# Layer 0 of a four-layer vision network: part of the second feed-forward product, the input transposes and the late norm are issued earlier within a strip

## The chip, the cores and the metric

The kernel runs on one core of a Trainium2 chip. The metric is the device time of one execution in microseconds (us); less is better. Each engine of the core works through its own queue of instructions in order: PE (TensorE, with PEld for its weight loads), DVE (VectorE), ACT (ScalarE), POOL (GpSimd) and SP (SyncE, which here issues most of the DMAs).

## The reference

Four layers run one after the other; each adds its result to its input. Everything is float32. The change touches layer 0 alone, a block with a depthwise convolution, a Mamba-2-like state-space mixer and a feed-forward part on 8 images of 64 x 64 positions and 192 channels:

```python
x = x + _L0_conv_ref(_gn(x), ...)     # layer 0: this case
x = x + _L1_conv_ref(_gn(x), ...)     # layer 1: four selective scans
x = x + _L2_conv_ref(_gn(x), ...)     # layers 2 and 3: 3x3 depthwise convolutions
x = x + _L3_conv_ref(_gn(x), ...)
```

Within layer 0, `_gn` normalizes over groups of 6 channels and the whole image, so its statistics are complete only when all of an image has been read. What follows, for each image:

- a 3x3 depthwise convolution, added to its input (conv1), and a layer norm over the channels (norm1);
- a projection to a gate z (384 columns), to x, B and C (512 columns) and to a time step dt for each of 6 heads (the "steps"); x, B and C pass a causal convolution over 4 positions and a silu, dt a softplus;
- the state-space sum in chunks: within a chunk `scores = (C B^T) * exp(seg) * dt` times x, and a state that is carried from chunk to chunk;
- the gate silu(z), an RMS norm and a projection back to 192 channels, added to the stream;
- a second 3x3 convolution (conv2), a second layer norm (norm2), and the feed-forward part: 192 to 768 channels, gelu, 768 to 192 channels, added.

## The kernel before, in words

**Tiling.** An image is cut into 8 strips of 512 positions (`NCH` = 8, `NJ` = 512); 8 images give 64 strips. Channels lie on the partitions as 2 groups of 96, positions in the free dimension. The chunk of the state-space sum is 128 positions, so a strip has 4 chunks (`NB` = 4).

**A pipeline over strips.** The loop at the end of `layer0` runs over q, and one turn of it (here "a strip") works on several strips at once, each at another stage: the first convolution and norm of strip q+1, the state-space part of strip q, the second convolution and norm of strip q-2, and the feed-forward part of strip q-3. The input of a strip nine ahead is transposed in the same turn (`take_in`, L237).

**What sets the order.** PE, DVE, ACT and POOL run in the order in which the Python code emits instructions; the order of SP's DMAs is left to the framework. The stages are generators that emit some instructions and then yield. `together` (L147) takes one step of each generator in turn, round after round, until those in its list are done; generators under `beside` get a step per round but aren't waited for. A generator that is listed twice gets two steps per round. So where a yield stands, and which generators are listed together, is the schedule.

**A turn has three phases.**

1. `widen` (first feed-forward product and gelu, L636), `project_xbc` (the x, B, C projection and its causal convolution, L387) and `project_out` of the strip before (L599), `conv1` (L314) and `residual` (L657) together. ACT needs the gelu table.
2. `gates` (L416): four matmuls of the gate projection, each with a silu on ACT, then the silu of B, C and x (L436 to L438), with one step of `conv2` (L629) per round beside them. ACT needs the silu table.
3. `exp_and_ln` loads a third ACT table (L693), and then `front` and `back` (the state-space part, chunk by chunk: L510 and L546), `narrow` (second feed-forward product, L664), the rest of `conv2`, and the chain `norms`: norm1, steps, norm2 and `take_in`, one after the other, two steps of it per round.

`norm2` can't begin before conv2 of its strip is done; it yields until then.

**Names and lines.** In `take_in`, L243 loads the input (SP), L249 transposes it (PE), L251 copies (ACT) and L252 takes bn_stats (DVE) of each half, L254 writes it out (SP); after the last strip of an image come the group norm's statistics (L259 to L276: bn_aggr, two small matmuls L263 and L271, a reciprocal root). `layer_norm` (L333) transposes to rows (L344), takes bn_stats (L349), computes 1/sqrt through Ln and Exp on ACT and four small DVE operations (`rsqrt`, L165 to L170), writes normalized rows (L357, ACT), transposes back (L369) and scales (L371). `steps` (L441) multiplies (L449), computes the softplus on ACT (L467 to L469), multiplies for cumulative sums (L477, L478), writes them to DRAM (L484) and reads them back broadcast to 128 partitions (L496); the relu of L506 in `exponents` reads these. In `front`, L524 to L527 transpose and multiply for a chunk, L529 is an exp, L532 copies x to positions on the partitions, L538 to L540 scale it on POOL, L541 multiplies the score matrix M. In `back`, L563 and L565 multiply with the state, L567, L570 and L571 update it, L574 and L576 multiply with M, L585 to L587 gate and square. In `narrow`, L677 multiplies six times for each half of the output channels into the one buffer of the PSUM bank "fc", L680 adds bias and residual (DVE, tile `xo`), L681 takes bn_stats, L682 stores (a DMA issued by POOL).

PSUM banks come from small rings by `bank`: two for "tp", two for "mm", three for "y", one for "fc". A matmul that would overwrite a bank waits until its last reader is done.

Of the kernel before, what the change touches and what calls it, by code (L numbers as in the profile page):

```python
# [15 lines left out]
B, H, W, C = 8, 64, 64, 192  # L16
# [10 lines left out]
NCH = L // NJ  # L27
# [119 lines left out]
def together(*threads, beside=()):  # L147

    threads = list(threads)
    while threads:  # L150
        for t in list(threads) + list(beside):
            if next(t, threads) is threads and t in threads:
                threads.remove(t)
# [20 lines left out]
def layer0(ctx: ExitStack, tc, a, dr, x, x1, mv1, cst):  # L174
# [58 lines left out]
    def at(q):  # L233
        return 0 <= q < len(strips)


    def take_in(b, r):  # L237
        if b >= B:
            return
        if r == 0:  # L240
            st0[b] = mk(pool, [CP, CT, NCH, 6], "st0")
        xt = mk(pool, [128, NB, C], "xt", bufs=2)
        nc.sync.dma_start(xt, x[b].rearrange("(g j p) c -> g p j c", p=128, j=NB)[r])  # L243
        xc = mk(pool, [CP, CT, NJ], "xc", bufs=2)
        yield
        for ct in range(CT):
            ps = bank("tp")[:CP]
            for j in range(NB):
                nc.tensor.transpose(ps[:, j * 128 : (j + 1) * 128], xt[:, j, ct * CP : (ct + 1) * CP], ident)  # L249
            yield  # L250
            nc.scalar.copy(xc[:, ct, :], ps)  # L251
            nc.vector.bn_stats(st0[b][:, ct, r, :], ps)  # L252
            yield
        nc.sync.dma_start(x0[b][:, :, r * NJ : (r + 1) * NJ], xc)  # L254
        if r < NCH - 1:
            return
        mv, d, q = (mk(pool, s, t) for s, t in (([CP, CT, 2], "mv0"), ([CP, CT], "gd"), ([CP, CT], "gq")))
        gm, sc, nb = (mk(pool, [CP, CT], t, bufs=2) for t in ("gm", "sc0", "nb0"))
        for ct in range(CT):  # L259
            nc.vector.bn_aggr(mv[:, ct, :], st0[b][:, ct, :, :])  # L260
        yield
        ps = bank("tp")[:CP, 0:CT]
        nc.tensor.matmul(ps, grp, mv[:, :, 0], start=True, stop=True)  # L263
        yield
        nc.vector.tensor_copy(gm, ps)
        nc.vector.tensor_tensor(d, mv[:, :, 0], gm, ALU.subtract)
        nc.vector.tensor_tensor(q, d, d, ALU.mult)
        nc.vector.tensor_tensor(q, q, mv[:, :, 1], ALU.add)
        yield
        ps = bank("tp")[:CP, 0:CT]  # L270
        nc.tensor.matmul(ps, grp, q, start=True, stop=True)  # L271
        yield
        nc.vector.tensor_scalar(q, ps, EPS, None, ALU.add)
        rsqrt(nc, pool, q, sc, "gr")
        nc.vector.scalar_tensor_tensor(nb, gm, -1.0, sc, ALU.mult, ALU.mult)
        norm[b] = sc, nb  # L276
        yield
# [96 lines left out]
    def norm1(q):  # L374
        if at(q):
            hn1[q] = mk(pool, [CP, CT, NJ], "hn1")
            yield from layer_norm(xs[q][:, :, W : W + NJ], l1w, l1b, hn1[q])

    def norm2(q):
        if at(q):  # L380
            while ("conv2", q) not in done:
                yield
            hn2[q] = mk(pool, [CP, CT, NJ], "hn2")
            yield from layer_norm(x2s[q], l2w, l2b, hn2[q])
# [31 lines left out]
    def gates(q):  # L416

        if not at(q):
            return
        zs = zss[q] = mk(pool, [128, NB, DIN], "zs")  # L420
        for i in range(NB):
            ps = bank("mm")
            for ct in range(CT):
                nc.tensor.matmul(
                    ps[:, 0:DIN],
                    hn1[q][:, ct, i * 128 : (i + 1) * 128],
                    w_zdt[:, ct, 0:DIN],
                    start=ct == 0,
                    stop=ct == CT - 1,
                )  # L430
            yield
            nc.scalar.activation(zs[:, i, :], ps[:, 0:DIN], AF.Silu)
        del hn1[q]
        cv = cvs[q]
        Bc, Cc = state["B"], state["C"] = mk(pool, [NS, NJ], "Bc"), mk(pool, [NS, NJ], "Cc")
        nc.scalar.activation(Bc, cv[0:NS, 3, :], AF.Silu)  # L436
        nc.scalar.activation(Cc, cv[NS:128, 3, :], AF.Silu)
        nc.scalar.activation(cv[:, 0:3, :], cv[:, 0:3, :], AF.Silu)  # L438
        yield
# [70 lines left out]
    def front(q, made):  # L510

        if not at(q):
            return
        dtv, E, _, _ = decays[q]
        cv, Bc, Cc = cvs[q], state["B"], state["C"]
        for i in range(NB):
            while made.get("back", 0) < i - 1:
                yield
            c0, c1 = i * 128, (i + 1) * 128
            if i + 2 < NB:  # L520
                fetch_sums(q, i + 2)
            ps = bank("mm")
            for o in range(DT):
                nc.tensor.transpose(ps[:, o * 128 : (o + 1) * 128], cv[:, o, c0:c1], ident)  # L524
            nc.tensor.transpose(ps[:, DIN : DIN + NS], Bc[:, c0:c1], ident[:NS, :NS])
            pgt = bank("mm")
            nc.tensor.matmul(pgt[:, 0:128], Bc[:, c0:c1], Cc[:, c0:c1], start=True, stop=True)  # L527
            M = made.pop(("M", i))
            nc.scalar.activation(M, M, AF.Exp, scale=-1.0)  # L529
            yield  # L530
            xb = mk(pool, [128, DIN + NS], "xb", bufs=2)
            nc.scalar.copy(xb, ps[:, 0 : DIN + NS])  # L532
            G = mk(pool, [128, 128], "G", bufs=2)
            nc.vector.tensor_tensor(G, pgt[:, 0:128], upper, ALU.mult)
            yield
            xv = split(xb[:, 0:DIN])
            xdt, xw, xd = (mk(pool, [128, DIN], t, bufs=2) for t in ("xdt", "xw", "xd"))
            nc.gpsimd.tensor_tensor(split(xdt), xv, heads(dtv[:, i, :]), ALU.mult)  # L538
            nc.gpsimd.tensor_tensor(split(xw), split(xdt), heads(E[:, 1, i, :]), ALU.mult)
            nc.gpsimd.tensor_tensor(split(xd), xv, heads(dsk), ALU.mult)  # L540
            nc.vector.tensor_tensor(M, M, G.unsqueeze(1).to_broadcast((128, NH, 128)), ALU.mult)  # L541
            made[i] = xb, xdt, xw, xd, M
            exponents(q, i + 1, made)
            yield
# [84 lines left out]
    def conv2(q):  # L629
        if at(q):  # L630
            x2s[q] = mk(pool, [CP, CT, NJ], "x2", bufs=2)
            yield from conv(xs[q], x2s[q], c2w, mid[:, 1, :], c2b)
            xs.pop(q - 1, None)
            done.add(("conv2", q))
# [29 lines left out]
    def narrow(q):  # L664
        if not at(q):
            return
        b, r = strips[q]
        sl = slice(r * NJ, (r + 1) * NJ)
        ff = ffs.pop(q)
        if r == 0:  # L670
            st1[b] = mk(pool, [CP, CT, NCH, 6], "st1", bufs=2)
        res = ress.pop(q)
        xo = mk(pool, [CP, CT, NJ], "xo")
        for ct in range(CT):
            ps = bank("fc")[:CP]
            for o in range(6):
                nc.tensor.matmul(ps, f2w[:, o, ct * CP : (ct + 1) * CP], ff[:, o, :], start=o == 0, stop=o == 5)  # L677
                if ct > 0 or o > 1:
                    yield
            nc.vector.scalar_tensor_tensor(xo[:, ct, :], ps, f2b[:, ct : ct + 1], res[:, ct, :], ALU.add, ALU.add)  # L680
            nc.vector.bn_stats(st1[b][:, ct, r, :], xo[:, ct, :])  # L681
        nc.gpsimd.dma_start(x1[b][:, :, sl], xo)  # L682
        if r == NCH - 1:
            for ct in range(CT):
                nc.vector.bn_aggr(mv1[:, b, ct, :], st1[b][:, ct, :, :])
        yield

    def one_by_one(*threads):
        for t in threads:
            yield from t  # L690
# [4 lines left out]
    with every_engine(tc):  # L695
        for r in range(NCH):
            if r == NCH - 1:
                exp_and_ln()
            together(take_in(0, r))
        load_strip(0)  # L700
        for q in range(-1, len(strips) + 3):
            load_strip(q + 2)
            load_residual(q - 2)
            together(
                widen(q - 3), one_by_one(project_xbc(q), project_out(q - 1)), conv1(q + 1), residual(q - 3)
            )
            made, second = {}, conv2(q - 2)
            exponents(q, 0, made)
            together(gates(q), beside=[second])
            exp_and_ln()  # L710
            norms = one_by_one(norm1(q + 1), steps(q + 1), norm2(q - 2), take_in(*divmod(q + NCH + 1, NCH)))
            together(front(q, made), norms, narrow(q - 3), back(q, made), norms, second)


@with_exitstack
# [602 lines left out]
```

## Time and profile before

| what | value |
|---|---|
| median of 3 runs | 26190.96 us (26157.72 to 26194.59) |
| the profiled execution | 26178.77 us, of which the span of its instructions is 26177.0 us |
| PE busy | 23676.9 us, 90% of the span |
| DVE busy | 22201.3 us, 85% |
| ACT busy | 20110.8 us, 77% |
| POOL busy | 17658.9 us, 67% |
| mean granted TensorE clock | 0.948 of full speed |

The span falls into stages: layer 0 up to about 5,690 us, layer 1's input part up to 8,600, its scans up to about 23,340, its output part up to about 24,640, then layers 2 and 3. The shares of the whole span are a mean over these, and the scans hold more than half of it; what a change in layer 0 is worth is read from layer 0's own part. "idle before" behind an instruction in the views is the time in which its engine had nothing running, with the engine, tile and line that ended it. The granted clock is the share of full TensorE speed that the chip's throttle gave in a stretch; in the trace of this case it is 1.0 or 0.5 at any moment.

### The profile page before, as it was taken

The page shows a single profiled execution, that of the slowest core. Times are in us where ns is not written, and L with a number is a line of the kernel's source. Part 1 is how long each engine was busy: PE and PEld are TensorE (multiplying, and loading weights), DVE is VectorE, ACT ScalarE, POOL GpSimd, SP SyncE. Part 2 cuts the span into 40 slices and gives each one's busy share as a digit, 9 for nine tenths or more (in the row PEclk, how much of TensorE's full clock was granted, in tenths as well). Part 3 has the DMA queues.
Part 4 walks back from the last instruction along what each step waited for, and adds up shares of the span by engine and source line. Part 5 has one row for each costly group of instructions (what it writes and reads, how often), then busy time and mean ns, then how long its engine had stood idle before and what let it go on. Part 6 is the DMA issues. An engine that isn't in the chain of part 4 may idle for free.

```text
span 26177.0 us, 442405 instructions
## 1 busy us (share of the span) xinstructions
PE 23676.9 (90%) x156160; PEld 18442.5 (70%) x156160; DVE 22201.3 (85%) x25001; ACT 20110.8 (77%) x40019; POOL 17658.9 (67%) x18396
## 2 busy tenths in 40 slices
PE   7888888888899999999999999999999999987766
PEld 4444444445588888888888888888888888863322
DVE  6777777756799999999999999999999999986566
ACT  4555555544499999999999999999999999974322
POOL 2222222210199999999999999999999999972100
PEclk8888888889999999999999999999999999998878
DMA  1111111113333333333333333333333333346311
GB/s 56 42 43 42 44 41 44 35 40 115 112 101 94 97 102 94 96 103 94 96 103 94 96 102 95 95 101 96 95 100 97 95 99 97 96 143 198 120 34 29
DMA packets 1461962, 2275.55 MB, mean 87 GB/s; under 512 B 247181, under 2 KB 773133, under 8 KB 1458202
## 3 DMA queue, kind: packets, MB, share of 16 engines
q1 hardware_dynamic: 1445402, 2196.90, 28.9%
q0 software_dynamic: 14336, 50.34, 0.5%
q8 instruction: 1232, 20.19, 0.3%
q14 instruction: 992, 8.13, 0.1%
HBM read 1811.37 MB, written 435.42 MB: 86 GB/s over the span
## 4 chain that ended last, share of the span: by engine, by line
PE 37%; ACT 29%; POOL 13%; DVE 13%; issue 6%; DMA 2%; POOLq 0%; SPq 0%; DVEq 0%; ACTq 0%
ACT dA L1045 12%; POOL hc L1095 10%; PE pd L1051 6%; ACT sb L1029 6%; PE yt L984 5%; DVE h L1086 5%; ACT bd L1029 4%; PE y L643 3%; PE fc L677 3%; DVE x L71 2%; PE pd L1053 2%; DMA yin<-y 2%; PE mm L399 2%; PE mm L943 2%; PE y L576 1%
## 5 line engine op out<-in xcount | busy, mean ns | idle before, releaser
L1095 POOL TENSOR_TENSOR hc<-h,bc 128x512 f32<-128x512 f32 x12288 | 15443.8, 1291 | 477.5 <-DVE h L1086 337.3
L1086 DVE TENSOR_TENSOR_SCAN h<-dA,st,pd 128x512 f32<-128x512 f32 x10752 | 12951.9, 1262 | 533.1 <-PE pd L1051 371.8
L1045 ACT ACTIVATE dA<-dl,A_logs 128x512 f32<-128x512 f32 x12288 | 8785.3, 715 | 46.9 <-DVE h L1086 39.6
L984 PE MATMUL yt<-sq,hc 128*128 128x128 f32 x49152 | 7489.9, 275 | 203.2 <-POOL hc L1095 102.8
L1051 PE MATMUL pd<-bd,dut 128*128 128x128 f32 x49152 | 6581.5, 277 | 254.2 <-DVE h L1086 232.1
L1051 PEld LDWEIGHTS pd<-bd,dut 128*128 128x128 f32 x49152 | 5968.6, 192 | 610.1 <-PE yt L984 342.9
L984 PEld LDWEIGHTS yt<-sq,hc 128*128 128x128 f32 x49152 | 5668.5, 141 | 649.3 <-POOL hc L1095 629.2
L1029 ACT ACTIVATE sb<-dut,xt 128x384 f32<-128x384 f32 x8192 | 4762.6, 606 | 1.1 <-DVE dut L970 1.0
L1053 PE MATMUL pd<-sq,sb 128*128 128x128 f32 x24576 | 3739.6, 275 | 9.3 <-DVE h L1086 0.4
L1053 PEld LDWEIGHTS pd<-sq,sb 128*128 128x128 f32 x24576 | 2821.8, 141 | 480.5 <-DVE dl L957 380.8
L1029 ACT ACTIVATE bd<-sq,xt 128x128 f32<-128x128 f32 x8192 | 3010.2, 392 | 0.0
L1086 DVE TENSOR_TENSOR_SCAN h<-dA,pd 128x512 f32<-128x512 f32 x1536 | 1772.8, 1203 | 115.4 <-PE pd L1051 75.8
L71 DVE SCALAR_TENSOR_TENSOR x<-x,w,x 96x3969 f32<-96x3969 f32 (+1 forms) x192 | 838.3, 4366 | 486.9 <-ACT x L64 483.9
L538 POOL TENSOR_TENSOR xdt<-xb,dtv 128x384 f32<-128x384 f32 x256 | 222.2, 868 | 1366.9 <-ACT xb L532 1366.8
L413 POOL COPY halo<-raw 128x12 f32<-128x12 f32 x64 | 13.0, 202 | 1375.7 <-ACT raw L403 1375.7
L304 DVE SCALAR_TENSOR_TENSOR x<-xs,cpe_w,x 96x504 f32<-96x504 f32 (+1 forms) x1024 | 902.1, 881 | 30.1 <-ACT x L292 20.3
L826 DVE SCALAR_TENSOR_TENSOR u<-xa,conv_w,u 128x504 f32<-128x504 f32 x1152 | 850.0, 742 | 50.2 <-ACT u L818 12.5
L943 PE MATMUL mm<-xs,w_dt 13*128 13x512 f32 x1536 | 863.0, 641 | 1.8 <-DVE dl L957 1.0
L677 PE MATMUL fc<-ff,fc_w 128*96 128x512 f32 x1536 | 861.0, 677 | 2.7 <-DVE xo L680 2.7
L1097 POOL COPY st<-h 128x3 f32<-128x3 f32 x4096 | 831.1, 203 | 0.0
L304 DVE SCALAR_TENSOR_TENSOR xs<-x0h,cpe_w,xs 96x504 f32<-96x504 f32 (+1 forms) x1024 | 757.8, 745 | 23.7 <-ACT xs L292 2.5
L643 PE MATMUL y<-hn,fc_w 96*128 96x512 f32 x1536 | 750.2, 627 | 0.1
(234 smaller groups left out, 25752.7 us busy)
## 6 DMA issues: line engine op xcount, KB each, us to landing
bc<-bcd SPq DMA_DIRECT2D x4096, 256.0 KB
yin<-y SPq DMA_DIRECT2D x256, 768.0 KB
csb<-csd SPq DMA_DIRECT2D x256, 384.0 KB
dut<-ut SPq DMA_DIRECT2D x128, 768.0 KB
y<-ys SPq DMA_DIRECT2D x128, 768.0 KB
dut<-ut SPq DMA_DIRECT2D x256, 384.0 KB
y<-ys SPq DMA_DIRECT2D x256, 384.0 KB
xt<-x1d SPq DMA_DIRECT2D x128, 384.0 KB
```

What stands on the lines that cost most here:

```text
L71: nc.vector.scalar_tensor_tensor(d[:, h0:h1, w0:w1], s[:, h0 + dy : h1 + dy, w0 + dx : w1 + dx], w[:, ct, tap : tap + 1], d[:, h0:h1, w0:w ...
L304: nc.vector.scalar_tensor_tensor(d[:, :, w0:w1], s[:, dy : dy + R, w0 + dx : w1 + dx], w[:, ct, tap : tap + 1], d[:, :, w0:w1], ALU.mult, ...
L643: nc.tensor.matmul(ps, f1w[:, ct, o * 128 : (o + 1) * 128], hn2[q][:, ct, :], start=ct == 0, stop=ct == CT - 1)
L677: nc.tensor.matmul(ps, f2w[:, o, ct * CP : (ct + 1) * CP], ff[:, o, :], start=o == 0, stop=o == 5)
L943: nc.tensor.matmul(ps, w_dt[:, k, o * 128 : (o + 1) * 128], made["xs"][0 : 1 + R1, :], start=True, stop=True)
L984: nc.tensor.matmul(yt[:, t * 128 : (t + 1) * 128], src[:, t * 128 : (t + 1) * 128], mat, is_transpose=mat is ident, start=first and t == 0 ...
L1029: nc.scalar.activation(v, src, AF.Copy, scale=m["xt"][:, t, 1 + R1 + n : 2 + R1 + n])
L1045: nc.scalar.activation(dA, ready[s]["dl"][:, o, :], AF.Exp, scale=aneg[:, k, o, n : n + 1])
L1051: nc.tensor.matmul(dst, ready[s]["dut"][:, t, cols], brows[g, t], start=True, stop=True)
L1053: nc.tensor.transpose(dst, brows[g, t][:, cols], ident)
L1086: nc.vector.tensor_tensor_scan(h[:, o, rev], decay.pop(j)[:, rev], turned.pop(j)[:, rev], 0.0 if first else st[:, o, n : n + 1], ALU.mult, ...
L1095: nc.gpsimd.tensor_tensor(hc, h[:, o, :], held[g], ALU.mult)
```

## The change

Five edits, all in layer 0:

- The group norm's statistics leave `take_in` and become a generator of their own, `statistics`.
- `take_in` moves from the end of the chain `norms` to phase 2, beside `gates`.
- In phase 2, `conv2` gets two steps per round instead of one.
- `narrow` yields for the first time after four matmuls instead of three, and its first step is taken ahead of phase 3, before ACT's table load; so four of the six matmuls of its first half stand before the first matmul of `front` on PE.
- In the chain `norms`, norm2 comes before the steps, and the statistics are last.

No instruction is added or dropped. Lines after L254 shift by 3.

```diff
@@ take_in
         nc.sync.dma_start(x0[b][:, :, r * NJ : (r + 1) * NJ], xc)
-        if r < NCH - 1:
+
+    def statistics(b, r):
+
+        if b >= B or r < NCH - 1:
             return
@@ narrow
                 nc.tensor.matmul(ps, f2w[:, o, ct * CP : (ct + 1) * CP], ff[:, o, :], start=o == 0, stop=o == 5)
-                if ct > 0 or o > 1:
+                if ct > 0 or o > 2:
                     yield
@@ the loops
-            together(take_in(0, r))
+            together(one_by_one(take_in(0, r), statistics(0, r)))
...
-            made, second = {}, conv2(q - 2)
+            made, second, ff = {}, conv2(q - 2), narrow(q - 3)
+            nxt = divmod(q + NCH + 1, NCH)
             exponents(q, 0, made)
-            together(gates(q), beside=[second])
+            together(gates(q), take_in(*nxt), beside=[second, second])
+            next(ff, None)
             exp_and_ln()
-            norms = one_by_one(norm1(q + 1), steps(q + 1), norm2(q - 2), take_in(*divmod(q + NCH + 1, NCH)))
-            together(front(q, made), norms, narrow(q - 3), back(q, made), norms, second)
+            norms = one_by_one(norm1(q + 1), norm2(q - 2), steps(q + 1), statistics(*nxt))
+            together(front(q, made), norms, ff, back(q, made), norms, second)
```

## The prediction

> **What bounds the kernel now.** I read the stages first (busy time by stretch), then the TensorE waits of the stage that the change touches, then one strip of that stage instruction by instruction. The columns of the first view are length, busy us (and instructions) of PE, PEld, DVE, ACT and POOL, granted clock, DMA share, GB/s.
>
> ```profile
> 133.00:5565.00 5432.00, 4609.30 (x16322) 2482.31 (x16321) 3842.20 (x7265) 2778.42 (x5895) 1466.70 (x1704) 0.86 0.13 41
> 8600.00:23340.00 14740.00, 14314.63 (x118151) 13040.23 (x118149) 14110.91 (x12795) 14387.04 (x29073) 14384.95 (x14898) 1.00 0.34 97
> ```
>
> Layer 0 is the first line: PE 85% busy, DVE 71%, ACT 51%, and a granted clock of 0.86 where the scan stage has 1.00. The change can act in these 5,432 us alone. The issues of L484, one per strip, stand 85.4 to 87.2 us apart in 45 strips (mean 85.9), 90 to 97 in eight, seven of them with an image's statistics, and 86.4 to 91.9 (mean 90.1) in the last seven, which have no transposes left to do. What PE waits for, between 400 and 5400 us (total us, times, longest):
>
> ```profile
> PE tp L369 <- ACT lrow L357: 361.2, 58, 6.5
> PE mm L524 <- ACT cv L438: 184.0, 57, 3.2
> PE y L574 <- POOL xd L540: 68.3, 57, 1.2
> PE y L565 <- POOL xw L539: 61.9, 57, 1.1
> PE tp L615 <- ACT yc L610: 35.5, 58, 0.6
> ```
>
> Two waits recur in every strip: 6.2 us for the rows of a layer norm, 3.2 us for the silu. One strip in order of time (start, us, engine, line, operation, idle before it) shows where:
>
> ```profile
> 2521.36 0.55 PE L524 MATMUL mm<-sq,cv 128*128 128x128 f32 x3 [3.23 <-ACT cv L438]
> 2523.37 5.33 PE L677 MATMUL fc<-ff,fc_w 128*96 128x512 f32 x6
> 2528.91 1.88 PE L677 MATMUL fc<-ff,fc_w 128*96 128x512 f32 x4
> ...
> 2560.64 2.66 PE L576 MATMUL y<-xdt,M 128*128 128x64 f32 x12
> 2563.09 1.49 PE L344 MATMUL tp<-sq,x 96*128 96x96 f32 x8
> 2570.81 2.11 PE L369 MATMUL tp<-sq,lrow 128*96 128x128 f32 x8 [6.22 <-ACT lrow L357]
> 2572.93 1.94 PE L249 MATMUL tp<-sq,xt 128*96 128x128 f32 x8
> 2574.66 2.78 PE L643 MATMUL y<-hn,fc_w 96*128 96x512 f32 x4
> ```
>
> The layer norm that ends the strip has nothing beside it: L344, bn_stats, rsqrt, rows and L369 follow one another. And matmuls run at half speed around both holes: six fc records took 5.33 us after the silu wait, where four took 1.88 later. Idle in this strip is 6.22 + 3.23 + 1.24 + 1.09 + 0.61 + 0.39 = 12.8 us of 87.0. Full-speed durations summed by line (24 fc records at 0.43, 24 of L643, 16 of L399, and so on) give 67 us of TensorE work; the other 6 to 7 us are the half clock.
>
> [...]
>
> **The change, part by part**, in strip time, t = 0 at the first L643 (2487.69). Lines are those of before.
>
> *Transposes into the silu phase.* Eight L249 records (1.73 us by their starts) go between the L424 products. L424 begins at t = 25.1 (2512.80): 25.1 + 5.33 + 1.73 = 32.2. On ACT one L251 copy (0.58) fits in the 0.80 us gaps between silus; the second copy and conv2's second identity (0.81) now stand before the table load, so the first xb comes about 2.2 us later. On DVE two bn_stats (0.69 each) join the convolution. On SP the xt load and the x0 write are issued mid-strip, strips ahead of their readers: nothing.
>
> *Four of the six fc steps of the first half before the front.* 8 x 0.43 = 3.4: PE reaches L524 at t = 35.6; the silu ends at 2521.3 + 1.05 = t 34.7. The 3.2 us wait is gone.
>
> *Two conv2 steps per round beside the gates.* DVE was already behind there; its row before shows the convolution running on past the silu, and the first xo far later:
>
> ```profile
> 2517.91 3.84 DVE L304 SCALAR_TENSOR_TENSOR x<-xs,cpe_w,x 96x504 f32<-96x504 f32 x5
> 2535.46 0.75 DVE L680 SCALAR_TENSOR_TENSOR xo<-fc,fc_b,res 96x512 f32<-96x512 f32 x1 [0.31 <-PE fc L677]
> ```
>
> Ten conv2 steps now precede the first bn_stats of norm1 instead of five.
>
> *The new wait.* The fc bank has one buffer. In the changed order PE has the second half's first fc step directly behind the first half's last, with both norm1 transposes already passed: it must wait until DVE has read the bank at L680, and DVE has that read after norm1's rsqrt chain and the first M product. PE is there at 35.6 + 1.0 (L524 to L527) + 2 x 0.45 (L344) + 2 x 0.86 (fc) = 39.2. DVE: first L405 at t = 6.5 (4.95 before; later because the last L587, the rms rsqrt, x0h 1.73 and the table load 1.28 now follow the last y product directly on ACT); 24.6 of conv work as before (2492.64 to 2517.91 less 0.8 of waits) = 31.1; 10 x 0.765 + 2 x 0.69 = 40.1; two stats pairs of 1.0, a conv step 0.7 and G 0.3 = 43.1; rsqrt and its hand-over 1.7 (2530.20 to 2531.75 plus ve) = 44.8; conv step, M, xo 0.7 + 0.9 + 0.7 = 47.1. PE idles about 8 us. Behind it stand L563, L565 and the second front group, and behind those the second xb, POOL's products and L570.
>
> *norm2 ahead of the steps.* The 6.2 us wait goes: norm2's DVE and ACT work falls among the third and fourth chunks. Late next is the fourth chunk: its xb copy stands on ACT behind norm2's rows, which wait for DVE. I count 1.4 + 0.5 (L369 for rows) + 1.1 (L565 for xw) = 3.0 us of idle, in place of the 2.3 for POOL. The steps then end the strip: L449 1.75, and L477 whose dA is ready about when L576 ends. Their csd write and csb reads move to the strip's end on SP; the first reader, L506, is at t = 20.3, and csd to csb took 1.4 us of issue before (2548.14 to 2549.52): hidden. On POOL the output DMA waits for the second xo ahead of the state product; I find it in time by under 1 us.
>
> *Sum.* From the new wait's end, t = 47.2: 28.8 of PE work, 3.0 idle, and half clock after an 8 us hole, 2.5 (bounds 1.7 to 3.4: four to seven us at half, as after the present holes) = 81.5 us. The unknown is the clock in the tail. Before, 1.1 + 1.2 us of idle near the end of a strip sufficed to halve it until some us into the next; the same would add 1.1 (at the start, the rest is taken out of the new wait) and 2.1 (at the end) = 84.7. Bounds 81.5 and 84.7; I take 83.6, nearer the second, since tail holes of that size halved it in every strip shown.
>
> Strips: 45 from 85.9 to 83.6, -104; the eight long ones, whose statistics chain stays as serial at the end, 2.3 each, -18; the last seven from 90.1 to 82.3 (1.4 us of bn_stats less ahead of the xo), -55. Sum -177; the few strips that fill the pipeline I leave. The profiled execution took 26,178.8 (span 26,177.0), giving 26,002; the median of the runs is 12 above it, so I predict **26,014**.
>
> **The rivals.**
> *The clock stays up and the wait is short* (25%): with fewer holes at the end the tail runs at 1.00, and DVE, with 29% idle, reaches the xo some us earlier. 80.3 a strip, -5.6 x 60 = -336: 25,855. For it: the 6.2 us hole is gone. Against: DVE's row is nearly closed from t = 5 to 47.
> *Nothing gained* (15%): the new 8 us wait stands for 6.2 + 3.2, the late strips stay as they are, POOL's products stretch in the tail (L540 took 2.14 us beside DVE work): 85.5, -0.4 x 60 = -24: 26,167.
> *Slower* (17%): the hole at the fc bank keeps the clock at half through the front, and the tail holes keep it there into the next strip. The last strips before show this price: 91.4 for less work than 85.4. From 2.9 us a strip over my forecast it decides; at 88.5, +2.6 x 60 = +156: 26,347.
> That the norm doesn't leave the tail I give no chance: the changed order has its transposes ahead of the steps' products.
>
> **How the numbers follow.** My case has 43%, its own range 25,900 to 26,130. The range 25,800 to 26,240 leaves out about a third of the first rival's cases and half of the third's. About 0.2% (52 us) is what a measurement of this kernel tells from no change: faster 0.67, same 0.15, slower 0.18.
>
> **What would show it.** Right: L369 and L524 vanish from PE's waits, and fc's matmul (L680 after) waits for xo (L683) by 6 to 9 us, 60-odd times; L484's successors stand 82 to 85 us apart; clock near 0.87. Wrong: no fc wait above 3 us (then faster); a clock below 0.83, or a tail with over 6 us of idle (then slower).

## The result, and the profile after

| | median us | against before, same chip |
|---|---|---|
| before | 26182.1 (4 executions) | |
| after | 26477.9 (4 executions, 26464.7 to 26482.6) | 1.0113, 95% interval 1.0096 to 1.0131 |

The change made the kernel 1.1% slower, about 296 us. The forecast was 26,014 us with a range up to 26,240: wrong in sign, and outside its range.

The first view of after is busy time by stretch, for layer 0 and for the scan stage (columns as before: length, busy us of PE, PEld, DVE, ACT and POOL with their instructions, granted clock, DMA share, GB/s).

```profile
133.00:5565.00 5432.00, 4734.19 (x15442) 2535.00 (x15442) 3533.47 (x6881) 2626.78 (x5585) 1232.65 (x1608) 0.79 0.13 39
8900.00:23640.00 14740.00, 14312.62 (x118129) 13037.06 (x118128) 14107.81 (x12794) 14391.00 (x29082) 14381.00 (x14893) 1.00 0.34 97
```

In the same 5,432 us PE ended 5% fewer instructions than before (15,442 against 16,322) and yet was busy 3% longer (4,734 against 4,609 us), at a granted clock of 0.79 instead of 0.86. The scan stage, which starts some 300 us later, takes what it took (POOL 14,381 against 14,385 us). So the loss is in layer 0, and it is not idle time (that fell from 823 to 698 us of the stretch): it is PE working at half speed. The clock row of the page, one digit for each fortieth of the span, has it too (before: eights in the first nine slices).

```profile
PEclk7877887789999999999999999999999999998888
```

The waits of PE between 400 and 5400 us (total us, times, longest):

```profile
PE fc L680 <- DVE xo L683: 440.5, 54, 8.3
PE tp L372 <- ACT lrow L360: 121.3, 54, 2.3
PE tp L618 <- ACT yc L613: 33.1, 54, 0.6
```

The two waits of before (6.2 us at the late norm, 3.2 us at the silu) are gone. In their place stand 8.2 us for the one fc bank and 2.2 us at the late norm. Below, a hole is a stretch in which PE waits, and the tail is the end of a strip, from the fourth chunk on. One strip in order of time, PE (start, us, line, operation, idle before it):

```profile
2489.56 1.02 PE L680 MATMUL fc<-ff,fc_w 128*96 128x512 f32 x2
2498.73 2.02 PE L680 MATMUL fc<-ff,fc_w 128*96 128x512 f32 x2 [8.14 <-DVE xo L683]
2500.68 1.64 PE L566 MATMUL y<-S,Cc 64*128 64x384 f32 x2
...
2523.49 1.45 PE L579 MATMUL y<-xdt,M 128*128 128x64 f32 x12
2527.18 2.10 PE L372 MATMUL tp<-sq,lrow 128*96 128x128 f32 x8 [2.24 <-ACT lrow L360]
...
2532.29 3.58 PE L452 MATMUL mm<-w_zdt,hn 96*128 96x6 f32 x16
...
2537.14 2.66 PE L579 MATMUL y<-xdt,M 128*128 128x64 f32 x12
2539.60 1.42 PE L480 MATMUL mm<-dA,sq 128*128 128x24 f32 x6
...
2541.50 3.78 PE L646 MATMUL y<-hn,fc_w 96*128 96x512 f32 x4
```

Compare equal records. (One float32 matmul of the kernel often stands as two records in the trace; an x2 or x12 in a line counts records.) Two fc records take 1.02 us ahead of the hole and 2.02 behind it; the twelve of L579 take 1.45 us in the middle and 2.66 behind the 2.24 us hole; L646, the first of the next strip, takes 3.78 us for four where full speed gives 1.88. The stretches from the hole's end to the end of the strip (columns of the first view):

```profile
2498.73:2511.00 12.27, 12.27 (x34) 6.18 (x35) 3.36 (x6) 2.05 (x4) 3.14 (x4) 0.55 0.00 0
2511.00:2525.00 14.00, 13.94 (x68) 7.91 (x66) 10.63 (x25) 8.01 (x22) 3.74 (x6) 1.00 0.02 2
2525.00:2541.50 16.50, 14.31 (x51) 10.19 (x51) 6.48 (x18) 5.21 (x14) 4.12 (x5) 0.56 0.15 47
2449.30:2498.73 49.43, 40.28 (x116) 18.82 (x115) 39.42 (x71) 29.66 (x58) 10.05 (x14) 0.88 0.20 59
```

In the first, PE has no idle time at all and still runs at 0.55 for 12.3 us. In the third, what there is of full clock falls in the 2.24 us in which PE waits; all its work, 14.31 us, is done at 0.5. Time times clock gives an estimate of the work at full speed: 12.27 x 0.55 + 13.94 + 14.31 x 0.5 = 27.8 us. The forecast had 28.8 us of work there. What it lacks is half clock, which cost 40.5 - 27.8 = 12.7 us.

Two figures describe each kernel below. "A strip" is the mean distance of the cumulative-sum writes (L484 before, L487 after) over 52 strips, those with an image's statistics included: 86.6 us before, 92.6 after. "Half" is the share of the time from 600 to 5000 us in which the clock record says 0.5: 0.257 before, 0.403 after.

### The profile page after: what moved, and what is told of

Its sections match the earlier page's. It is cut to its first block, busy times and chain, and to the rows that moved or that the text cites. A ratio compares the mean times of both kernels' runs of the same rounds, so it can differ in the third digit from the quotient of the medians.

```text
span 26472.9 us, 442561 instructions
## 1 busy us (share of the span) xinstructions
PE 24057.8 (91%) x156160; PEld 18628.4 (70%) x156160; DVE 22076.0 (83%) x25001; ACT 20103.1 (76%) x40019; POOL 17505.3 (66%) x18396
## 4 chain that ended last, share of the span: by engine, by line
PE 33%; ACT 26%; DVE 19%; POOL 13%; issue 7%; DMA 2%; POOLq 0%; SPq 0%; DVEq 0%; ACTq 0%
ACT dA L1050 11%; POOL hc L1100 11%; ACT sb L1034 6%; PE pd L1056 6%; DVE h L1091 5%; PE yt L989 5%; ACT bd L1034 4%; PE y L646 3%; DVE x L71 2%; DVE x L307 2%; DVE xs L307 2%; DMA yin<-y 2%; PE pd L1058 2%; PE fc L680 2%; PE mm L948 2%
## 5 line engine op out<-in xcount | busy, mean ns | idle before, releaser
L307 DVE SCALAR_TENSOR_TENSOR x<-xs,cpe_w,x 96x504 f32<-96x504 f32 (+1 forms) x1024 | 804.5, 790 | 41.4 <-ACT x L295 22.1
L646 PE MATMUL y<-hn,fc_w 96*128 96x512 f32 x1536 | 823.6, 678 | 0.0
L680 PEld LDWEIGHTS fc<-ff,fc_w 128*96 128x96 f32 x1536 | 239.2, 180 | 708.5 <-DVE xo L683 549.5
```

The costliest lines, as they stand in the source:

```text
L307: nc.vector.scalar_tensor_tensor(d[:, :, w0:w1], s[:, dy : dy + R, w0 + dx : w1 + dx], w[:, ct, tap : tap + 1], d[:, :, w0:w1], ALU.mult, ...
L646: nc.tensor.matmul(ps, f1w[:, ct, o * 128 : (o + 1) * 128], hn2[q][:, ct, :], start=ct == 0, stop=ct == CT - 1)
```

## The experiments

In the ratios each kernel stands against the kernel before on the same chip. The theory at the start: the waits came as forecast, and what made the kernel slow is the half clock behind them. The rivals: the changed chain itself is longer (PE starts later on everything behind the fc bank), or one of the other edits costs.

### Filling the hole with useless matmuls

From after, nine matmuls of no use (18 records) go in front of the second half; their result isn't read.

```diff
             nc.vector.bn_stats(st1[b][:, ct, r, :], xo[:, ct, :])
+            if ct == 0:
+                idle = bank("y")[:CP]
+                for _ in range(9):
+                    nc.tensor.matmul(idle, f2w[:, 0, 0:CP], ff[:, 0, :], start=True, stop=True)
```

> The changed kernel, with nine extra 128x512 matmuls per strip (about 7.7 us of TensorE work at full speed) put where TensorE waits for the fc bank; their result is overwritten unread. Clock theory (the hole of 8 us halves the clock for five 3.4 us windows, and about 11 us of real matmuls behind it run at half speed): useless work makes the kernel faster, by 4 to 6 us a strip, to 86 to 88 us a strip and about 26,100 to 26,250 us; the matmuls behind the hole go back to 0.43 us a record. Chain theory (a strip is bound by the row of dependent work on DVE, ACT and POOL, and TensorE's speed doesn't decide): 92 us a strip as before or a little more, 26,470 to 26,550 us.

Measured: 26166.9 us, ratio 1.000 (0.999 to 1.001). With 7.9 us more PE work in each strip it is 310 us faster than after; a strip 87.3 us, half 0.217. PE in one strip:

```profile
2445.17 7.89 PE L688 MATMUL y<-ff,fc_w 128*96 128x512 f32 x18
2453.47 1.10 PE L680 MATMUL fc<-ff,fc_w 128*96 128x512 f32 x2 [0.41 <-DVE xo L683]
2454.50 0.91 PE L566 MATMUL y<-S,Cc 64*128 64x384 f32 x2
...
2476.69 2.10 PE L372 MATMUL tp<-sq,lrow 128*96 128x128 f32 x8 [2.24 <-ACT lrow L360]
...
2481.80 3.58 PE L452 MATMUL mm<-w_zdt,hn 96*128 96x6 f32 x16
```

PE gets past the fc bank hardly earlier than in after (48.8 us into the strip by the median of 600 to 5000 us, 49.4 in after), but what follows takes 1.10 and 0.91 us, not 2.02 and 1.64. The tail, which wasn't filled, is at half as in after. So a longer chain isn't what costs: with the bank passed at nearly the same time, keeping the clock up behind it gives back some 5 us a strip.

### Taking the hole away: the second half later, or the fc steps as before

```diff
 # second half two rounds later
+            for _ in range(2 if ct == 0 else 0):
+                yield
 # or: fc as in the kernel before, all other edits kept
-                if ct > 0 or o > 2:
+                if ct > 0 or o > 1:
...
-            next(ff, None)
```

> The changed kernel, but the second half of the second feed-forward product is held back two rounds, so that its first matmul stands behind the first chunk's y products and no longer waits for xo. Bank theory (the wait for the one fc bank costs the time): the wait of 8 us goes, the y products start some us earlier, 84 to 87 us a strip, 26,000 to 26,150 us. Rival (DVE's row is late anyway, so TensorE waits nearly as long one step later, for the first M product or for xw): a wait of 4 to 6 us at L577 or L568 in its place, the clock still halves, 89 to 92 us a strip, 26,300 to 26,450 us.

> The changed kernel without the early part of the second feed-forward product (three matmuls before the first yield, none ahead of the front). Bank theory: the silu wait is back at about 2.5 us, the fc wait is gone, the last wait stays at about 2.3 us; 83 to 86 us a strip, 25,950 to 26,150 us: the early part is what makes the change slow. Rival (the transposes and the second conv2 step load DVE too early, whatever TensorE does): a wait of several us for M or the norm instead, 89 to 92 us a strip, 26,300 us or more.

Measured: 25663.9 us, ratio 0.9806 (0.9778 to 0.9835), a strip 79.2, half 0.188; and 25667.1 us, 0.9808 (0.9779 to 0.9836), 79.5, half 0.182. Both are faster than before and after, and some 300 us below the lower range expected: the sign was the bank theory's, the size was in neither. In the first, the fc wait is all but gone (3 us in the whole of layer 0); what remains is a wait for rows of a norm in the front. Keep the second line for later: 4.1 us behind the wait L372 is at full speed again.

```profile
2410.33 1.25 PE L372 MATMUL tp<-sq,lrow 128*96 128x128 f32 x4 [3.70 <-ACT lrow L360]
...
2414.43 0.60 PE L372 MATMUL tp<-sq,lrow 128*96 128x128 f32 x4
```

So the early fc part by itself costs 811 us on top of the other edits (26477.9 - 25667.1), and the other edits together gain 1.9%. The gain was there; the fc bank gave it back and more.

### Three parts one by one

```diff
 # after, with one conv2 step per round
-            together(gates(q), take_in(*nxt), beside=[second, second])
+            together(gates(q), take_in(*nxt), beside=[second])
 # before, with norm2 ahead of the steps alone
-            norms = one_by_one(norm1(q + 1), steps(q + 1), norm2(q - 2), take_in(...))
+            norms = one_by_one(norm1(q + 1), norm2(q - 2), steps(q + 1), take_in(...))
 # before, with the early fc matmuls alone
-                if ct > 0 or o > 1:
+                if ct > 0 or o > 2:
...
+            next(ff, None)
             exp_and_ln()
```

> The changed kernel with one conv2 step per round beside the gates, as before. DVE then reaches the first norm five steps of 0.77 us earlier. Bank theory: the fc wait falls from 8 to 4 to 5 us. But conv2 ends later, and norm2, now ahead of the steps, must wait for it: norm2 and the steps end the strip one after the other. If the tail decides more than the fc wait: a wait of 6 us for rows is back and one for dA beside it, 92 to 96 us a strip, 26,450 to 26,700 us. If the fc wait decides: 86 to 89, 26,100 to 26,300 us.

> The kernel before, with norm2 ahead of the steps and nothing else of the change. If norm2's place by itself is worth something: the 6.2 us wait for rows shrinks and strips fall to 80 to 83 us, 25,850 to 26,050 us. If conv2, with one step per round, ends too late for it (as the fourth experiment suggests): norm2 and then the steps and the transposes stand at the end of a strip, 90 to 94 us, 26,450 to 26,700 us.

> The kernel before, with only the early part of the second feed-forward product. The silu wait of 3.2 us goes. By DVE's row as I read it (five conv2 steps and two bn_stats fewer ahead of the first norm than in the changed kernel, 5.2 us) TensorE waits about 3 us for xo, the same hole at another place: 85 to 87 us a strip, 26,130 to 26,280 us. If the early part is harmful by itself, as large as in the changed kernel: a wait of 8 us, 90 us a strip or more, 26,450 us or more.

Measured: 26708.0 (1.0205, 1.0176 to 1.0235; a strip 96.5); 26495.0 (1.0124, 1.0095 to 1.0154; 92.7); 26369.9 (1.0089, 1.0058 to 1.0119; 90.5). The first is 8 us above its upper range, the second inside the range of its second case, the third between its two. Without the second conv2 step the late norm waits again, and the fc wait doesn't fall as far as expected; PE's waits of that kernel between 400 and 5400 us:

```profile
PE tp L372 <- ACT lrow L360: 326.8, 52, 6.8
PE fc L680 <- DVE xo L683: 299.8, 52, 5.8
```

Norm2's new place alone costs 1.2%: it has to wait for conv2, and now the steps wait behind it. Early fc alone brings an fc wait of 5.7 us a time, between what the two theories had said (3 and 8 us), and costs 0.9%.

### Does the tail answer to the same cure?

From the kernel with the second half two rounds later: eight useless matmuls ahead of the steps' products, or the second half held for six rounds, so that its fc matmuls fall into the tail.

```diff
 # fill
         pdt = bank("mm")
+        for _ in range(8):
+            nc.tensor.matmul(pdt, w_xbc[:, 0, 0:128], hn1[q][:, 0, :], start=True, stop=True)
 # hold
-            for _ in range(2 if ct == 0 else 0):
+            for _ in range(6 if ct == 0 else 0):
```

> The second experiment with eight extra 128x512 matmuls (6.9 us at full speed) ahead of the products of the steps at the end of each strip, their result overwritten unread. Clock theory: the tail's thin matmuls (128x6, 128x64) don't keep the clock up; with dense ones among them the half-clock run of three windows at the strip's end goes, and the extra 6.9 us are nearly paid back: 79 to 82 us a strip, 25,700 to 25,850 us, L577 and L579 in the tail at full speed. If the tail's clock doesn't depend on what TensorE does there: 86 us a strip, 26,090 us or more.

> The second experiment with the second half held back six rounds instead of two, so that its last matmuls stand in the tail between the products of the steps. Real dense work in the tail: if it keeps the clock up and covers the waits there, 75 to 77 us a strip, 25,500 to 25,620 us. If the front then lacks it (the wait for the first norm's rows grows and halves the clock there): 79 to 82 us, 25,700 to 25,900 us.

Measured: 26043.4 (0.9958, 0.9939 to 0.9978; a strip 85.3, half 0.153) and 26022.9 (0.9942, 0.9920 to 0.9965; 84.0, half 0.311). Both are slower than the kernel that they start from, so both expectations of the time failed.

The filling does act on the clock: in the strip that I had looked at in the kernel it starts from, the steps' product took 2.97 us and M's 2.66; with the filling (first line) the product takes 1.84.

```profile
2443.59 1.84 PE L454 MATMUL mm<-w_zdt,hn 96*128 96x6 f32 x16
```

```profile
2433.45 2.97 PE L452 MATMUL mm<-w_zdt,hn 96*128 96x6 f32 x16
2437.69 2.66 PE L579 MATMUL y<-xdt,M 128*128 128x64 f32 x12
```

But one strip doesn't stand for all. Two other strips of the kernel without the filling, at their start:

```profile
2363.31 1.98 PE L646 MATMUL y<-hn,fc_w 96*128 96x512 f32 x4
2685.45 1.98 PE L646 MATMUL y<-hn,fc_w 96*128 96x512 f32 x4
```

From 600 to 5000 us, 24 of its 56 strips start like these, at full clock, and 32 at about 3.78; with the filling 17 of 51 are still slow. In all, the half clock falls from 14.9 us a strip (0.188 x 79.2) to 13.1 (0.153 x 85.3), which is worth about 1 us, and for that the filling pays 7.1 us in every strip (eight matmuls, by the trace): 6.1 us a strip slower. I had taken one strip for all.

The held kernel's tail was at full clock (last line of the next view), but it lost elsewhere. It took fc matmuls out of the front, and there stands the 3.70 us wait for L372, which the kernel that it starts from has as well:

```profile
2448.19 1.25 PE L372 MATMUL tp<-sq,lrow 128*96 128x128 f32 x4 [3.70 <-ACT lrow L360]
...
2450.51 2.66 PE L579 MATMUL y<-xdt,M 128*128 128x64 f32 x12
...
2460.11 2.66 PE L579 MATMUL y<-xdt,M 128*128 128x64 f32 x12
...
2482.63 1.45 PE L579 MATMUL y<-xdt,M 128*128 128x64 f32 x12
```

```profile
2448.19:2475.00 26.81, 26.81 (x83) 15.93 (x84) 14.93 (x35) 12.62 (x32) 10.73 (x12) 0.52 0.00 1
```

After that one wait PE is never idle for 26.8 us, and runs at 0.52. In the first 15.6 us of it there is no matmul of 512 columns. Twelve records of 64 columns take 2.66 us at half and 1.45 at full clock. But in the strip shown of the kernel with two rounds the same L372, L577 and L579 follow the same wait, and there full speed was back within 4.1 us, ahead of any 512 columns. So a dense matmul directly behind the hole is not the whole of it; what the matmuls of the two counted behind it is in the last section.

### What the gain is made of

Early fc out in all of these. First the transposes and conv2 without norm2's new place (after, with the fc lines as before and `steps` ahead of `norm2`); and the changed kernel with its fc matmuls spread in another way:

```diff
-                if ct > 0 or o > 2:
+                if ct > 0 or o > 0:
```

> Two parts of the change alone: the input transposes beside the gates and two conv2 steps per round. The fc matmuls are where they were before, and norm2 comes after the steps again. Theory (the clock decides, and a hole at the strip's tail costs its length and the half clock behind it): the transposes fill the silu wait (3.2 us to about 1.5), but norm2 ends the strip again with its 6 us wait for lrow, now without the transposes behind it; so little is gained: 84 to 87 us a strip, 26,070 to 26,250, and the step from here to the kernel with all but the early fc (25,667) belongs to norm2's place. Rival: these two parts carry the gain of that kernel by themselves (silu wait gone, conv2 early enough for norm2 to run beside the last chunks): 79 to 81 us a strip, below 25,800.

> The changed kernel with two of the first half's fc matmuls ahead of the front and the other four one per round, instead of four and two. Theory (what costs is the hole at the one fc bank and the half clock after it): the second half's first matmul comes two rounds later, when xo's operands are ready, so the wait for xo falls below 2 us or goes, and the dense fc matmuls stand among the thin ones of the first chunks: 76 to 79 us a strip, 25,520 to 25,680, the fastest so far. Rival: the instruction that reads the bank and the matmul that overwrites it are still issued directly behind one another, so PE waits for xo at the later place as well (over 4 us): 85 us a strip or more, above 26,100.

Measured: 25659.8 (0.9804, 0.9790 to 0.9819; a strip 79.6, half 0.163) and 25718.1 (0.9827, 0.9810 to 0.9843; 80.1, half 0.188). In the first the rival was right: these two edits carry the whole gain, and norm2's new place adds nothing that can be told from noise (25667.1 with it). In the second the fc wait is gone as the theory had it, but the norm's wait in the front stays at 3.7 us, and the time missed its range by 38 us. Then each of the two edits on the kernel before:

```diff
 # conv2 alone
-            together(gates(q), beside=[second])
+            together(gates(q), beside=[second, second])
 # transposes alone
+            together(gates(q), take_in(*nxt), beside=[second])
```

> The kernel before with one word added: conv2 gets two steps per round beside the gates instead of one. Theory: this is what makes the two-part run (transposes and conv2, 25,660) fast, since conv2 then ends early enough that norm2's wait at the strip's tail falls from 6.2 us to below 4; most of the gain stays: 80 to 82 us a strip, 25,770 to 25,900. Rival: the silu wait (3.2 us) and the transposes at the tail stay, the clock is at half around both, and the gain needs the transposes' move: 84 us a strip or more, above 26,050.

> Only the input transposes move to the gates (with the statistics' generator); conv2 has one step per round, norm2 follows the steps and the fc matmuls are as before. Theory: norm2 waits for conv2 as before, and without the transposes behind it the tail is barer: lrow waits of 6 us or more, 85 to 88 us a strip, 26,100 to 26,300. Rival: the transposes take the silu hole (3.2 us falls below 2) and the clock at half behind it goes: 82 us a strip or less, below 25,920.

Measured: conv2 alone 25781.9 (0.9853, 0.9837 to 0.9870; a strip 81.6, half 0.173), as expected; transposes alone 26386.5 (1.0081, 1.0066 to 1.0096; 90.5, half 0.343), above its range, though with the expected wait. The late norm and the next strip's start, in the conv2 kernel and then in the transposes' one:

```profile
2513.71 1.04 PE L369 MATMUL tp<-sq,lrow 128*96 128x128 f32 x8
...
2518.05 1.45 PE L576 MATMUL y<-xdt,M 128*128 128x64 f32 x12
2520.21 1.88 PE L643 MATMUL y<-hn,fc_w 96*128 96x512 f32 x4
```

```profile
2484.54 2.66 PE L579 MATMUL y<-xdt,M 128*128 128x64 f32 x12
2494.70 2.11 PE L372 MATMUL tp<-sq,lrow 128*96 128x128 f32 x8 [6.21 <-ACT lrow L360]
2496.82 3.78 PE L646 MATMUL y<-hn,fc_w 96*128 96x512 f32 x4
```

With two conv2 steps per round the norm no longer ends the strip: its transpose stands between the chunks without a wait, the tail runs at full clock, and the next strip starts at full clock (1.88 us, not 3.78). The silu wait of 3.23 us is still there in that kernel. So the norm's hole was worth far more than the silu's.

One more pair is in these traces. In the conv2 kernel the front too has a norm wait, of 3.38 us; there two fc records follow 1 us behind it:

```profile
2488.95 1.25 PE L369 MATMUL tp<-sq,lrow 128*96 128x128 f32 x4 [3.38 <-ACT lrow L357]
2489.99 1.91 PE L677 MATMUL fc<-ff,fc_w 128*96 128x512 f32 x2
...
2495.14 0.60 PE L369 MATMUL tp<-sq,lrow 128*96 128x128 f32 x4
```

Full speed is back 6.2 us behind the wait, against 26.8 us in the kernel that had held its fc matmuls.

The parts, added up in this order (medians; the kernel before was 26,164 to 26,182 us in these series):

| edit | alone on before | added in turn |
|---|---|---|
| conv2 twice per round | -388 us | -388 us |
| transposes beside the gates | +217 us | -122 us |
| norm2 ahead of the steps | +331 us | +7 us |
| early fc matmuls | +206 us | +811 us |

The edits don't add: alone they would sum to +366 us, in turn they sum to +308. Three kernels (25,660 to 25,667 us) are the fastest, and these runs don't tell them apart.

## Why the prediction was wrong

**The waits were right.** The silu wait went. The fc bank's wait was forecast at about 8 us for the reason given (one buffer, the reader behind norm1's chain) and measured at 8.1 to 8.3. In it PE ran no later matmul ahead of the one that waited (8.14 us with nothing running, at 2498.73). It ended at 49.4 us in the strip (2449.35 to 2498.73) where the forecast had 47.2. The tail's idle was 2.2 us, forecast 3.0. All of it was for the late norm's rows, where 1.9 had been forecast; the 1.1 us for xw didn't come. The work left behind the hole was 27.8 us, forecast 28.8. The moved copies brought no table load: each of the three loads of a strip stands 54 times between 400 and 5400 us (L650, L435, L696), 57 or 58 times in before. In before the copies of L251 stand between the third load (L693) and the next strip's first (L647), under the table of exp; in after between the second (L435) and the third (L696), beside silu.

**The step that failed is "half clock after an 8 us hole, 2.5 (bounds 1.7 to 3.4)" with its companion for the tail, "2.1 (at the end)".** From the hole's end to the strip's end the forecast has 28.8 + 3.0 + 2.5 + 2.1 = 36.4 us (83.6 less 47.2); measured are 42.8 (2498.73 to 2541.50), where half clock cost 12.7 us for 4.6. That is 8.1 us too little, less 0.8 of idle and 1.0 of work that didn't come; with the 2.2 us by which the fc wait ended late it makes the whole gap between 83.6 and 92.2 us.

The bounds were drawn from the kernel before: "four to seven us at half, as after the present holes". But close behind the silu hole of before stood six fc records of 512 columns, and behind the norm's hole, after 3.9 us of transposes of 128 columns, stood L643, again 512 columns. The changed order put matmuls of fewer columns behind both holes: ahead of the fc bank it had used up four of the six fc matmuls, and in the tail it had put the steps' products (6 columns) and M's (64 columns) where the transposes had been, directly before L643. Behind the first hole the clock was back after 11.1 us (2498.73 to 2509.87), behind the second after 20 us (2527.18 to 2547.42). I counted the holes and not what stands behind them.

No run shows 2.5 us as the price of an 8 us hole; in after the clock stood at half for 17.1 us about it (2492.81 to 2509.87), 11.1 of them with PE at work. Nor did the length of a hole or the busy time behind it give the price in these traces. PE was busy without a gap for 12.3 us at a granted 0.55 in after, and for 26.8 us at 0.52 in the kernel that had held its fc matmuls. And the clock fell with the 2.24 us hole of the tail, as it had in before with the 3.23 us of the silu and with 1.09 + 1.24 us in the tail. What the matmuls counted while it stood at half is in the last section.

**The parts were valued in the wrong order.** The forecast saw conv2's second step only as ten DVE steps ahead of the norm. It is the edit that makes the gain: alone -1.5%. Norm2's new place, from which I took the 6.2 us, gives nothing once conv2 is early, and without it costs 1.2%. The transposes, taken as a fill for the silu hole, cost 0.8% alone.

**The rivals.** "Slower" named what decided: half clock behind the fc bank (0.55 over 12.3 us), and from the tail into the next strip (2526.94 to 2547.42). Its price, 88.5 us a strip, was still 3.7 under the 92.2 measured. It had 17%, because its evidence, the last strips before with 91.4 us "for less work than 85.4", was noted and not followed up. "The clock stays up and the wait is short" comes near in number to the kernel whose second half starts two rounds later (79.2 a strip, forecast 80.3). "Nothing gained" had the late strips right and no price for the clock. The last seven strips, forecast to fall from 90.1 to 82.3, stayed at 90.4. The signs named beforehand came true on the wrong side: an fc wait in its range, but 92 us between strips and a clock of 0.79 in layer 0 against the limit of 0.83.

## What to carry to other kernels

Where an engine's clock falls behind a hole, price the hole with its length and with the half speed behind it, and look which matmuls stand there: in the strips shown full speed was back 4.1 and 6.2 us behind a wait in two kernels, about 12 and 27 us behind one in two others, and the last section has what the matmuls counted. Moving dense work ahead of a wait to fill it takes that work from the place behind the next wait. And before a chain's end is reordered, ask what it waits for: conv2, one step more per round, did what the new order of the norms could not.

## What the hardware showed that I had not expected

- Useless matmuls made the kernel faster: 7.9 us of them per strip in the place of an 8.1 us hole gave 310 us.
- PE at half clock while never idle, for up to 26.8 us (0.52, second half six rounds later). In the traces of before and after, from 600 to 5000 us, the changes of the clock stand whole multiples of 3.41 us apart. So I cut the time between them into windows of that length, and counted in each what the matmuls move: a record whose second shape is KxN counts N x K / 128 columns (512 for an fc record, 192 for L566, 64 for one of L579, 4.5 for one of L452), spread over its time up to the next record's start. Set against 1,530 columns, the 2,580 windows of the two traces are:

| clock in the window | columns | windows | followed by half clock | followed by full clock |
|---|---|---|---|---|
| half | below 1,530 | 647 | 647 | 0 |
| half | 1,530 or more | 210 | 8 | 202 |
| full | below 1,530 | 202 | 202 | 0 |
| full | 1,530 or more | 1,521 | 1 | 1,520 |

Windows behind four holes, from the one in which PE starts again:

| kernel | columns in the windows at half clock |
|---|---|
| after, from 2496.22 | 484, 1360, 1507, 1902, then full clock |
| second half six rounds later, from 2446.54 | 946, 1344, 1313, 1476, 1186, 1453, 1393, 1918, then full clock |
| second half two rounds later, from 2410.26 | 1627, then full clock |
| conv2 alone, from 2487.99 | 1361, 1534, then full clock |

- Busy time doesn't say it: of the 518 half-clock windows of before and after in which PE was busy for 99% or more, 199 were followed by full clock, and none of these had fewer than 1,530 columns. In the strip of after shown above, the first four full-clock windows behind the hole of the table's first row count 2,522 to 3,192 columns; half of that, an estimate for the same work at half clock, is 1,261 to 1,596, on both sides of 1,530. The 1,530 was fitted to these traces afterwards, and no run varied the shape of the matmuls alone: that this count is what sets the clock was not shown.
- Strips settle on steps of about 3.41 us, the unit of the clock records in before and after (half and full periods last whole multiples of it, 17.07 and 34.13 us among them): of 63 strip distances 38 in after, 27 with norm2 alone and 24 with the transposes alone are 92.1 to 92.2 us, 27 x 3.413 = 92.15; 33 with early fc alone are 88.7 to 88.8, 26 x 3.413 = 88.7; 18 of before are 85.4 to 85.5, 25 x 3.413 = 85.3. In the faster kernels the commonest distance is now at such a multiple (78.5, 23 x 3.413, nine times with the second half two rounds later) and now off it (77.7, 17 times, with the transposes and conv2). Why a strip should settle on it was not tried.
